# Two graph-attention layers on one core: the last scores moved behind the first attention, and one product given a bank of its own

## The chip, the core and the metric

The kernel runs on one core of a Trainium2 chip. The metric is the device time of one execution in microseconds (us), as the median of several runs. All times below are us unless they are marked ns. The engines are TensorE (PE for matmuls, PEld for loading the stationary operand), VectorE (DVE), ScalarE (ACT), GpSimd (POOL) and SyncE (SP). SP and ScalarE both issue transfers.

## The reference, cut to what matters

There are 64 graphs of 256 nodes with 512 features. The first layer mixes the features of each graph's nodes with a softmax over masked sums, and the second is an attention with 8 heads, biased by the logarithm of the adjacency.

```python
# layer 0
feat_proj = einsum('bnh,oh->bno', feats, fc_w) + fc_b
logits = q + swapaxes(k, 2, 1)                  # q, k: one number per node
masked = logits + (1.0 - adj_mat) * NEG_INF
masked = where(masked >= 0, masked, 0.01 * masked)
x1 = einsum('bnm,bmh->bnh', softmax(masked), feat_proj) + feats
# layer 1, heads of 64
Q, K, V = x1 @ W_q + b_q, x1 @ W_k + b_k, x1 @ W_v + b_v
scores = einsum('bihd,bjhd->bhij', Q, K) / sqrt(64)
scores = scores + soul_bias + log(adjacency + 1e-9)
out = einsum('bhij,bjhd->bihd', softmax(scores), V) + x1
```

Everything is float32.

## The kernel before

**Groups and steps.** Two graphs make a group (512 tokens), and there are 32 groups. The kernel is a software pipeline over groups: one `step` works on up to four of them at once. `d` is the group whose outputs are being finished, `a` the one in layer 1's attention, `f` the one that goes through layer 0's last part and the projections Q, K and V, and `n` the next one, for which weights of layer 0 are prepared. The function `attention_and_layer_0` holds the first half of a step and exists in 31 of the 32 steps. The order of the work is written out by hand as strings of names, each naming a method of a group: `A("scores:2 attend:0")` calls `scores(2)` and `attend(0)` of group `a`. Each engine, and the queue of transfers on SP and on ScalarE, executes its own instructions in exactly the order in which these calls issue them.

**Products.** Each of the four 512x512 projections (`pf` with fc_w, `pq`, `pk`, `pv`) is done by a scheme with seven products of half-size blocks (p1 to p7) in place of eight. A product is four matmuls of 128x128 by 128x256 (`add`, L412). They accumulate in few PSUM banks: in `r` products 1, 6, 5 and 3 follow each other, and between them ScalarE copies the partial sums to SBUF (`keep`). For `pf` (class `Mixed`), `keep` multiplies by the reciprocal of a softmax sum on ScalarE (L494) and POOL then adds the old x (L495). `sum` (L501 in `Mixed`, L443 elsewhere) adds a bank to what was kept and writes one quarter of the result, on VectorE: `sum_00`, `sum_11`, `sum_01`, `sum_10`. For `pf` the result is x1, written over x.

**The way of x1 to TensorE.** The projections need x1 transposed. Each quarter (o,k) of x1 goes this way. `send:o:k` transposes 32x32 blocks on VectorE into `xt` (L771) and writes `xt` to a scratch tensor `xd` in device memory by one transfer of 256 KB on SP (L775). `fetch:o:k` reads it back in a permuted order into `x1T` by four transfers of 64 KB on SP (L789), and `fetch_by_both:0:1` issues two of its four on ScalarE. `copy:0` copies the quarter (0,0) of `x1T` into `t1b_c` on ScalarE (L378), and `pv.p1` uses this copy as its stationary operand. `xsum:0` to `xsum:3` write the differences of quarters that products 4 to 7 need (`t1b`, L375, VectorE). `pq.p6` needs the second one, `xsum:1`, and that needs the quarters (0,0), (0,1) and (1,1).

**Layer 1's attention.** A group has four pieces of scores (u = 0 to 3, two for each graph). `scores:u` computes them (L843), and ScalarE applies the exponential (L857, `e`, six buffers). `factor:u:j` multiplies by the adjacency (L863, VectorE), and `both:u` adds two tiles for the softmax sums (L870). `attend:g` multiplies by V of graph g (L883), and `totals_g` sums (L910). The matmuls of scores have a contraction of 64, those of attend and totals 64 output rows; two of them share the array at a time. In the page's rows their operands read 64*128 and 128*64, against 128*128 for a product. The text calls a run of such matmuls between products a divided cluster. `turn`, `ratios`, `divide`, `complete` and `store` finish the output; `parts` prepares the sums. `keys` computes four rows of dot products of x1 on VectorE (L516), after which `load_x` may overwrite x with the next group's (SP, L206).

**PSUM.** Four banks are handed out by `bank` and two pairs of banks by `pair`, which scores and product 7 of `pq` use. A tile gets a bank once its last user has released it, so a matmul that starts a tile waits for the engine that read the bank last.

Of the kernel before, what the change touches and what calls it, by code (L numbers as in the profile page):

```python
# [25 lines left out]
def kernel(  # L26
# [86 lines left out]
    both = [i for i, a in enumerate(act_sets.SETS) if a.name == "natural_log_exp_and_others"]  # L113
# [50 lines left out]
    def fast():  # L164
        main = ExitStack()
        with main:
# [222 lines left out]
            class Product:  # L389
# [5 lines left out]
                scores = False  # L395
# [75 lines left out]
                def p3(self):  # L471
                    self.add(3, self.r, False)
                    self.read(self.out(0, 1), self.r, 0)
# [7 lines left out]
            class Mixed(Product):  # L481
# [22 lines left out]
                        )  # L504

                def p3(self):
                    self.add(3, self.r, False)

                def sum_01(self):
                    self.sum(0, 1, self.r, self.out(0, 1))  # L510


            def dot_rows(src, w_row, init, dst, name):
# [526 lines left out]
            def attention_and_layer_0(D, A, F, X, check):  # L1040

                A("scores:0")
                D("attend:1 totals_1")
                F("add_tiles")
                A("scores:1 factor:0:0 factor:0:1 pv.sum_11 pv.p3 pv.p4")
                D("ratios:1 turn:1")
                F("parts_0")
                A("factor:1:0 factor:1:1 pv.sum_10 both:0 both:1")
                check()
                F("mix:0 mix:1 ysum:0 recip")  # L1050
                D("divide:1 complete:1 store:1")
                A("residual:1")
                F("mix:2 mix:3 ysum:1 ysum:2 ysum:3")
                A("parts:0")
                F("pf.p1 pf.keep_1 pf.p2 pf.p6 pf.sum_00 begin send:0:0 fetch:0:0")
                A("turn_residual:1 parts:1")
                F("pf.p7 pf.p5")
                A("scores:2 attend:0 totals_0")
                F("pf.sum_11 send:1:1 fetch:1:1")
                A("factor:2:0 factor:2:1 turn:0")  # L1060
                F("pf.p3 pf.sum_01 send:0:1 pq.p1 pq.keep_1 copy:0 fetch_by_both:0:1")
                A("ratios:0 both:2")
                F("pf.p4 pf.sum_10 send:1:0")
                A("scores:3")
                F("fetch:1:0")
                A("factor:3:0")
                F("pk.p1 pk.keep_1 pv.p1 pv.keep_1")

            def check_ranges():

                in_range(NG - NR // 2, NG, "last")
                pk = bank("pok")
                nc.tensor.transpose(pk[0:1, 0:P], checked["all"], ident)

                def flag_ready():
                    oks = one.tile([1, 2], F32, tag="oks", name="oks")
                    nc.vector.tensor_reduce(oks[:, 0:1], pk[0:1, 0:P], AX.X, ALU.min)
                    nc.vector.tensor_copy(flag, oks[:, 0:1])

                return flag_ready  # L1080
# [3 lines left out]
            def step(d, a, f, n, check):  # L1084


                def of(group):
                    def issue(pieces):
                        for piece in pieces.split():
                            name, *args = piece.split(":")  # L1090
                            if group is None:
                                continue
                            target = group
                            if "." in name:
                                part, name = name.split(".")
                                target = getattr(group, part)
                            getattr(target, name)(*map(int, args))
                    return issue

                D, A, F, X = of(d), of(a), of(f), of(n)  # L1100
                X("load_adj")
                if a is not None:
                    attention_and_layer_0(D, A, F, X, check)
                else:
                    f.features_first()
                    F("pq.p1 pq.keep_1 copy:0 pk.p1 pk.keep_1 pv.p1 pv.keep_1")
                F("xsum:0 xsum:1 xsum:2 pq.p6 keys:2 keys:3 keys:0 keys:1")
                X("load_x")
                A("factor:3:1 both:3")
                F("pq.p7 pq.p2 pq.sum_00 xsum:3 pq.p5 pk.p6 pq.sum_11 pq.p3")  # L1110
                A("divide:0")
                X("dot_q:0 dot_q:1 dot_q:2 dot_q:3 spread")
                F("pq.p4 pq.sum_10 copy:1 copy:2")
                A("complete:0 store:0 parts:2")
                if n is None:
                    A("parts:3")
                F("pk.p7 pk.p5 pk.sum_11 residual:0")
                X("adjt")
                F("pk.p2 pk.sum_00")
                X("dot_k:0 dot_k:1")  # L1120
                F("pk.p3 pk.p4 pk.sum_10")
                X("dot_k:2 dot_k:3")
                F("turn_residual:0")
                if n is None:
                    A("attend:1 totals_1 ratios:1 turn:1 divide:1 complete:1 store:1")
                    F("residual:1 turn_residual:1")

                    F("pv.p2 scores:0 pv.p6 pv.sum_00 factor:0:0 factor:0:1 scores:1 both:0 pv.p7")
                    F("factor:1:0 factor:1:1 both:1 scores:2 pv.p5 sums_1:0 scores:3 pv.sum_11")
                    F("ratios_t:0 ratios_r:0 factor:2:0 factor:2:1 pv.p3 pv.p4 factor:3:0 pv.sum_10")  # L1130
                    F("factor:3:1 attend:0 finish:0 sums_of_e:1 attend:1")
                    F("ratios_t:1 ratios_r:1 finish:1")
                    check_ranges()()
                    return
                X("mask add_eps")
                F("pv.p2 pv.p6")
                X("weights:0")
                F("pv.p7 pv.p5")
                X("weights:1")
                F("pv.sum_00")  # L1140
                A("parts:3")

            with tc.manual_schedule(engines=ENGINES):
                f = Group(0)
                f.x, f.a = x_0, adj_0

                warm = bank("warm")
                for n in range(6):
                    nc.tensor.matmul(warm[:, 0:P], lhsT=ident, rhs=ident, start=True, stop=True)
                columns(rows_0, cols_0, "cols_0")  # L1150
                rows_qk = rows_of_x()
                k_constant = constant()
                d, a, a_w = None, None, {}
                for g in range(NG):
                    n = Group(g + 1) if g + 1 < NG else None

                    def check():

                        if d is not None and (d.g % NR == NR - 1 or d.g == NG - NR // 2 - 1):
                            in_range(d.g // NR * NR, d.g + 1, f"{d.g}")  # L1160

                    step(d, a, f, n, check)
                    d, a, f = a, f, n
# [215 lines left out]
```

## Time and profile before

| | before |
|---|---|
| median of 3 runs | 2327.16 (2326.76 to 2327.59) |
| profiled execution, its own time | 2324.43 |
| span of the profiled execution | 2322.6 |
| TensorE clock granted | 0.998 of full |
| TensorE with a matmul under way | 2302.7 (99%) |
| VectorE busy | 2092.7 (90%) |
| ScalarE busy | 1071.0 (46%) |
| POOL busy | 122.0 (5%) |
| DMA engines, mean busy share of q1 and q10 | 28.5% and 0.8% |

In the profile a matmul's recorded end overlaps the start of the next, so its cost is read from one start to the next. A float32 matmul appears as two records of PE and two of PEld. A row of the timeline gives the start, the duration of the merged records, the engine, the line, the operation and its tiles; in brackets stands how long the engine was idle before it, and what ended that. SPq and ACTq are the issue of transfers.

### The profile page before, as it was taken

Reading aid. Unit: us, or ns where it says so; the run is one execution under the profiler, and the core shown is the slowest. Engines: PE = TensorE matmul, PEld = TensorE weight load, DVE = VectorE, ACT = ScalarE, POOL = GpSimd, SP = SyncE. Lnnn points to the kernel's source line nnn. Section 1 sums busy time; section 2 is a strip of 40 time slices with the busy share of each in tenths; the row PEclk is TensorE's granted clock in tenths of the full one; section 3 lists DMA queues with packets and bytes.
Section 4 is the critical chain, followed back from the end, with each engine's and each line's share of the span. In section 5 each row is a group of like instructions: output and inputs, shape, how many; then the busy total and the mean of one; then the engine's idle time right before and its main releaser. Section 6 shows DMA issues by size and latency. Waiting matters only on the chain.

```text
span 2322.6 us, 33706 instructions
## 1 busy us (share of the span) xinstructions
PE 2302.7 (99%) x12738; PEld 1906.0 (82%) x12738; DVE 2092.7 (90%) x3088; ACT 1071.0 (46%) x1865; POOL 122.0 (5%) x120
## 2 busy tenths in 40 slices
PE   9999999999999999999999999999999999999997
PEld 5888888888888888888888888888888888888885
DVE  6799889999899998999999999999999989999897
ACT  3544445444444444454444444444544445444443
POOL 0000000000000000000000000000000000000000
PEclk9999999999999999999999999999999999999999
DMA  4122323223322323232233223322222323323312
GB/s 132 48 59 72 78 75 67 64 66 84 79 73 56 68 73 78 73 69 60 69 80 84 64 61 67 80 78 73 64 60 73 78 74 68 64 64 85 79 46 38
DMA packets 517263, 163.84 MB, mean 71 GB/s; under 512 B 415188, under 2 KB 478696, under 8 KB 517096
## 3 DMA queue, kind: packets, MB, share of 16 engines
q1 hardware_dynamic: 505512, 156.25, 28.5%
q10 hardware_dynamic: 11584, 5.38, 0.8%
q8 instruction: 103, 1.69, 0.3%
q14 instruction: 64, 0.52, 0.1%
HBM read 95.43 MB, written 66.12 MB: 70 GB/s over the span
## 4 chain that ended last, share of the span: by engine, by line
PE 95%; DVE 2%; DMA 2%; issue 0%; ACT 0%; ACTq 0%; DVEq 0%
PE pv L412 17%; PE pq L412 16%; PE pk L412 16%; PE pf L412 16%; PE sc L843 10%; PE oT L883 10%; PE y L667 9%; DMA x1T<-xd 1%; DMA xd<-xt 1%; PE fp L696 1%; DVE t1b L375 0%; DMA fc_nat<-in_L_gnn_fc_w_dram 0%; PE tot L910 0%; DVE xt L771 0%; PE rc L621 0%
## 5 line engine op out<-in xcount | busy, mean ns | idle before, releaser
L863 DVE TENSOR_TENSOR e<-e,am 128x1024 f32<-128x1024 f32 x254 | 300.5, 1214 | 24.1 <-ACT e L857 24.1
L857 ACT ACTIVATE e<-sc,c 128x1024 f32<-128x1024 f32 x254 | 269.0, 1110 | 77.0 <-PE sc L843 73.5
L843 PE MATMUL sc<-qT,kT 64*128 64x256 f32 x2048 | 255.8, 389 | 0.4 <-ACT e L857 0.4
L883 PE MATMUL oT<-e,v 128*64 128x256 f32 x2032 | 233.4, 382 | 0.0
L495 POOL TENSOR_TENSOR pf_s<-pf_s,x 128x512 f32<-128x512 f32 x93 | 118.5, 1274 | 2118.7 <-ACT pf_s L494 1673.4
L843 PEld LDWEIGHTS sc<-qT,kT 64*128 64x128 f32 x2048 | 187.2, 186 | 51.5 <-issue 31.5
L667 PE MATMUL y<-e,x 128*128 128x256 f32 x992 | 226.1, 382 | 0.0
L883 PEld LDWEIGHTS oT<-e,v 128*64 128x64 f32 x2032 | 140.2, 137 | 85.4 <-issue 21.3
L432 ACT ACTIVATE pq_s<-pq,cols 128x256 f32<-128x256 f32 x192 | 80.5, 470 | 279.1 <-PE pq L412 279.1
L667 PEld LDWEIGHTS y<-e,x 128*128 128x128 f32 x992 | 186.1, 190 | 24.0
L494 ACT ACTIVATE pf_s<-pf,recip 128x256 f32<-128x256 f32 x186 | 77.9, 470 | 197.6 <-PE pf L412 197.6
L900 DVE TENSOR_REDUCE part<-est 128x32 f32<-128x1024 f32 x124 | 151.3, 1220 | 4.3
L899 DVE STREAM_TRANSPOSE est<-es 128x1024 f32<-128x1024 f32 x124 | 152.2, 1227 | 0.0
L870 DVE TENSOR_TENSOR es<-e,e 128x1024 f32<-128x1024 f32 x126 | 149.3, 1205 | 1.1
L673 ACT COPY yT<-y 128x512 f32<-128x512 f32 x124 | 72.6, 586 | 131.5 <-PE y L667 130.8
L890 ACT COPY oTs<-oT 128x512 f32<-128x512 f32 x128 | 75.0, 586 | 119.1 <-PE oT L883 98.4
L429 ACT COPY pk_s<-pk 128x512 f32<-128x512 f32 x96 | 56.3, 586 | 151.9 <-PE pk L412 151.9
L412 PE MATMUL pk<-x1T,wk 128*128 128x256 f32 x512 | 124.2, 385 | 0.0
L412 PE MATMUL pk<-t1b,wk 128*128 128x256 f32 x512 | 121.1, 379 | 0.4 <-DVE kT L443 0.4
L412 PE MATMUL pv<-wv,t1b_c 128*128 128x256 f32 x512 | 121.1, 379 | 0.0
L412 PE MATMUL pv<-wv,t1b 128*128 128x256 f32 x512 | 121.1, 379 | 0.0
L412 PE MATMUL pq<-x1T,wq 128*128 128x256 f32 x512 | 121.0, 379 | 0.0
(180 smaller groups left out, 4474.7 us busy)
## 6 DMA issues: line engine op xcount, KB each, us to landing
x<-in_x_dram SPq DMA_DIRECT2D x32, 1024.0 KB, 5.1
out_dram<-osb SPq DMA_DIRECT2D x254, 128.0 KB, 3.3
xd<-xt SPq DMA_DIRECT2D x124, 256.0 KB, 2.0
x1T<-xd SPq DMA_DIRECT2D x434, 64.0 KB, 1.9
adj<-in_adj_dram SPq DMA_DIRECT2D x128, 128.0 KB, 3.5
qrow<-q SPq DMA_DIRECT2D x31, 256.0 KB, 3.9
x1T<-xd ACTq DMA_DIRECT2D x62, 64.0 KB, 2.4
fc_nat<-in_L_gnn_fc_w_dram ACTq DMA_DIRECT2D x4, 256.0 KB, 3.8
```

Source lines behind the costliest of these rows:

```text
L412: nc.tensor.matmul(o, lhsT=lk[:, ts(m, P)] if len(lk.shape) == 2 else lk[:, m], rhs=rk, start=(start and m == 0 and k == 0), stop=(m == 1 ...
L432: nc.scalar.activation(dst[:, m], src[:, m], AF.Identity, bias=self.bias[:, 2 * o + m : 2 * o + m + 1],)
L494: nc.scalar.mul(s[:, m], src[:, m], self.recip[:, TPG * k + m : TPG * k + m + 1])
L495: nc.gpsimd.tensor_tensor(s, s, self.out(o, k), ALU.add)
L667: nc.tensor.matmul(y[:, ts(gr, N)], lhsT=self.x[:, gr * TPG + j, ts(c, P)], rhs=self.e0[:, j, gr, :], start=(gr == 0 and j == 0), stop=(gr ...
L843: nc.tensor.matmul(sc[:, par, pr, :], lhsT=self.kT[rows, 2 * hg + pr, ts(t, P)], rhs=self.qT[rows, 2 * hg + pr, ts(gr, N)], start=True, st ...
L857: nc.scalar.activation(e, sc, AF.Exp, bias=self.c[:, t : t + 1], scale=SCALE)
L863: nc.vector.tensor_tensor(ef, ef, self.am[:, jc, u // 2, :].unsqueeze(1).to_broadcast([P, 4, N]), ALU.mult,)
L870: nc.vector.tensor_tensor(self.esum[u], self.e[u, 0], self.e[u, 1], ALU.add)
L883: nc.tensor.matmul(oT[par * HD : (par + 1) * HD, pr, :], lhsT=self.v[:, gr * TPG + jc, ts(h, HD)], rhs=self.e[2 * gr + hg, jc][:, par, pr, :],
L899: nc.vector.transpose(turned, self.esum[u].rearrange("p a b i -> p (a b i)"))
L900: nc.vector.tensor_reduce(self.part[:, hg, :], turned.rearrange("p (m c) -> p m c", c=B), AX.X, ALU.add,)
```

## The change

Three things are edited, all in the order of a step.

1. `pf.p3` no longer accumulates onto `r`, but starts a bank of its own, `r3`, and moves from behind `totals_0` to directly behind `pf.p5`, ahead of `scores:2`. The quarter (0,1) of x1 then takes two passes of `sum`: `add_01` adds the bank `r`, and `sum_01` adds `r3`. `add_01` stands ahead of `sum_11`.
2. `scores:3` moves up from behind `pf.p4` to directly behind `totals_0`. `pf.p4`, `pq.p1`, `pk.p1` and `pv.p1` follow it without another cluster between them. With this move `fetch_by_both:0:1` stands ahead of `scores:3` and of `pq.keep_1` and `copy:0` on ScalarE, where it had stood behind `copy:0`. `sum_01 send:0:1` move ahead of `factor:2:0` on VectorE, `send:1:1 fetch:1:1` ahead of `scores:2`.
3. `factor:3:0`, `factor:3:1` and `both:3` now stand together behind `xsum:2` and ahead of `keys`. Before, `factor:3:0` stood ahead of `xsum:0`, and the other two behind `keys`.

```diff
                 def p3(self):
-                    self.add(3, self.r, False)
+                    self.r3 = self.fresh(3)
+
+                def add_01(self):
+                    self.sum(0, 1, self.r, self.out(0, 1))
 
                 def sum_01(self):
-                    self.sum(0, 1, self.r, self.out(0, 1))
+                    self.sum(0, 1, self.r3, self.out(0, 1))
...
                 A("turn_residual:1 parts:1")
-                F("pf.p7 pf.p5")
+                F("pf.p7 pf.p5 pf.p3 pf.add_01 pf.sum_11 send:1:1 fetch:1:1")
                 A("scores:2 attend:0 totals_0")
-                F("pf.sum_11 send:1:1 fetch:1:1")
-                A("factor:2:0 factor:2:1 turn:0")
-                F("pf.p3 pf.sum_01 send:0:1 pq.p1 pq.keep_1 copy:0 fetch_by_both:0:1")
-                A("ratios:0 both:2")
-                F("pf.p4 pf.sum_10 send:1:0")
-                A("scores:3")
-                F("fetch:1:0")
-                A("factor:3:0")
-                F("pk.p1 pk.keep_1 pv.p1 pv.keep_1")
+                F("pf.sum_01 send:0:1 fetch_by_both:0:1")
+                A("factor:2:0 factor:2:1 scores:3 turn:0 ratios:0 both:2")
+                F("pf.p4 pf.sum_10 send:1:0 fetch:1:0")
+                F("pq.p1 pq.keep_1 copy:0 pk.p1 pk.keep_1 pv.p1 pv.keep_1")
...
-                F("xsum:0 xsum:1 xsum:2 pq.p6 keys:2 keys:3 keys:0 keys:1")
+                F("xsum:0 xsum:1 xsum:2 pq.p6")
+                A("factor:3:0 factor:3:1 both:3")
+                F("keys:2 keys:3 keys:0 keys:1")
                 X("load_x")
-                A("factor:3:1 both:3")
                 F("pq.p7 pq.p2 pq.sum_00 xsum:3 pq.p5 pk.p6 pq.sum_11 pq.p3")
```

## The prediction

> **What bounds the kernel.** I read the busy table first, then TensorE's waits, then one undisturbed step of the timeline, engine by engine.
>
> ```profile
> PE 2302.7 (99%) x12738; PEld 1906.0 (82%) x12738; DVE 2092.7 (90%) x3088; ACT 1071.0 (46%) x1865; POOL 122.0 (5%) x120
> PE pq L412 <- DVE t1b L375: 3.3, 6, 1.3
> q8 instruction: 103, 1.69, 0.3%
> ```
>
> TensorE has work in 99% of the span, so a gain must come from its own instruction stream, or from its few waits. The list of waits holds one that recurs: six times the pq product 6 waits for a difference of x1 pieces (t1b), which waits for a transfer. TensorE's timeline of one step, and next to it ScalarE's, SP's and VectorE's:
>
> ```profile
> 740.53 1.89 PE L412 MATMUL pf<-fcT,tb 128*128 128x256 f32 x8
> 742.35 2.00 PE L843 MATMUL sc<-qT,kT 64*128 64x256 f32 x16
> 744.28 3.67 PE L883 MATMUL oT<-e,v 128*64 128x256 f32 x32
> 747.78 0.26 PE L910 MATMUL tot<-part,every 128*64 128x32 f32 x4
> 747.97 1.99 PE L412 MATMUL pf<-fc_s,yT 128*128 128x256 f32 x8
> 749.80 1.89 PE L412 MATMUL pq<-x1T,wq 128*128 128x256 f32 x8
> 751.53 1.89 PE L412 MATMUL pf<-fcT,tb 128*128 128x256 f32 x8
> 753.35 2.00 PE L843 MATMUL sc<-qT,kT 64*128 64x256 f32 x16
> 755.28 1.99 PE L412 MATMUL pk<-x1T,wk 128*128 128x256 f32 x8
> 757.11 1.89 PE L412 MATMUL pv<-wv,t1b_c 128*128 128x256 f32 x8
> ```
> ```profile
> 751.73 0.84 ACT L432 ACTIVATE pq_s<-pq,cols 128x256 f32<-128x256 f32 x2 [3.14 <-PE pq L412]
> 752.46 0.62 ACT L378 COPY t1b_c<-x1T 128x512 f32<-128x512 f32 x1
> 753.72 0.85 ACTq L789 DMA_DIRECT2D x1T<-xd  x2
> 754.62 2.12 ACT L857 ACTIVATE e<-sc,c 128x1024 f32<-128x1024 f32 x2 [1.55 <-PE sc L843]
> ```
> ```profile
> 746.33 0.34 SPq L775 DMA_DIRECT2D xd<-xt  x1
> 748.40 1.73 SPq L789 DMA_DIRECT2D x1T<-xd  x4
> 751.65 0.34 SPq L775 DMA_DIRECT2D xd<-xt  x1
> 753.72 0.78 SPq L789 DMA_DIRECT2D x1T<-xd  x2
> ```
> ```profile
> 744.68 0.88 DVE L501 SCALAR_TENSOR_TENSOR x<-pf,recip,pf_s 128x256 f32<-128x256 f32 x2 [0.89 <-POOL pf_s L495]
> ```
>
> (q8: packets, MB, share of the DMA engines.) See in TensorE's rows the distance from start to start, since ends overlap. A product takes 1.73 (749.80 to 751.53). The last product before a divided cluster takes 1.82 (740.53 to 742.35), the first one after it 1.83 (747.97 to 749.80). So each divided cluster costs 0.09 + 0.10 = 0.20 at its edges (0.198 from the records in ns). Most steps repeat every 71.16.
>
> **What the Trainium skill says.** The Trainium skill, "TensorEngine Tiling (Array Packing)", Key Properties: a change of tiling mode drains TensorE. The 0.09 and 0.10 agree. The same skill, "PSUM — Partial Sum Buffer", Engine vs sequencer instructions: ScalarE's queue is a strict FIFO. In the fourth step of this trace ScalarE stands 3.46 behind one late xd transfer, with the exponentials of the scores behind it. And "Runtime: NRT & Kernel Launch", Instruction fetch mechanics: instructions come by DMA in 16 KiB blocks of 256, mostly hidden. Here q8's packets are 16,384 bytes, some 23 us apart, one per 256 TensorE records; they are hidden from TensorE, but not from transfers in flight, as shown below.
>
> **The change, part by part.** Everything is laid on the clock of the step above.
>
> 1. Two clusters instead of three. After: p5 740.53, p3 742.26, scores 2 744.08, attend 746.01, totals 749.51, scores 3 749.70, p4 751.63, pq.p1 753.46, pk.p1 755.18, pv.p1 756.91, pq.p6 758.64 (758.83 before). No matmul is added or removed; one cluster's edges go: 31 steps x 0.198 = **-6.1**.
>
> 2. The banks. p3 takes a bank that TensorE itself freed. attend then needs VectorE's sum_00 (done 739.5, needed 746.0) and the new add_01 (744.65, needed 747.8), totals needs sum_01 (747.1, needed 749.5), scores 3 needs the exponentials of scores 2 (746.3 and 747.4, needed 749.7). Margins of 2 us and more: 0.
>
> 3. add_01: two more VectorE instructions of L501, 0.88 a pair. They run from 743.8 to 744.65, inside the 0.89 in which VectorE waits for POOL. Without that cover send:1:1 would be 0.9 later. Cost 0; sum_11 and its transposition stay at 744.68 and 745.59.
>
> 4. Differences before the last factors. xt of piece (0,1) is ready at 747.85 instead of 751.6. SP, however, issues in order: the four fetches of (1,1) end at 750.13, so xd follows at 750.17, only 1.5 earlier than before. It lands 2.06 later, 752.2; the fetches land by 755.1, and the second difference, for which pq.p6 waits, is done at 756.6 instead of 758.3, with 1.8 to spare instead of 0.5. The six waits, 4.3 and 0.10 of restart each by the records, should go: **-4.9**.
>
> 5. factor:3 and both:3 ahead of keys: VectorE ends keys at 763.5 instead of 761.7, and load_x on SP starts 1.75 later. It lands 5.1 later, 768.7, where VectorE wants it at 768.4. The 0.3 is lost in the 1.1 that the first kT sum has before pk.p4 needs it. Cost 0, at most 0.1 a step.
>
> 6. ScalarE's place for the two fetches. Before they stood behind pq.keep_1 and copy:0, and ahead of scores 3 only. Now they stand ahead of the exponentials of scores 3, pq.keep_1 and copy:0, and **pv.p1 loads its weights from what copy:0 writes**. ScalarE waits until 752.2, issues for 0.85, and runs the exponentials 753.12 to 755.24; it can take pq.keep_1 at 755.15, where pq.p1 is done at 755.38: **0.24 to spare**. Then copy:0 ends at 755.38 + 1.35 = 756.73 (751.73 to 753.08 took 1.35), and pv.p1 can bear a load up to 756.80, less 0.05 of signalling (both seen where TensorE waited for VectorE). In a quiet step this costs 0, by 0.02.
>
> 7. In a step that isn't quiet, xd of (0,1), or the transfers of (1,1) ahead of it on SP, are late, and nearly all of it reaches TensorE. Set against the times of q8's packets, the late transfers are those that met one. Twelve xd writes that did so took 0.9 to 2.0 more than 2.06 (mean 1.3); five sets of four fetches took 0.5 to 1.5 more to issue (mean 0.9). The exposed stretch now runs from xd of (1,1) to ScalarE's second fetch, 746.3 to 753.1. By TensorE's records it holds some 115 of 256, as small matmuls go by fast there: 115/256 x 31 = 14 steps. At 0.9 (hits at the edges cost less) minus 0.2 to spare: 14 x 0.7 = **+9.8**. Bounds: the delays that this trace has on the same transfers, less the slack, give 7.0 with half of the stretch empty; I take 5 as the low end, and 15 x 1.15 = 17 as the high end.
>
> Sum: -6.1 - 4.9 + 9.8 = -1.2. The profiled execution took 2324.4 (span 2322.6); it would take 2323.2. The median of the runs is 2.7 higher, so I forecast **2326.0**. About 0.2%, 4.65 us, is what a measurement of this kernel can tell from no change.
>
> **Rivals.**
> (a) Likeliest: gains and ScalarE's new wait cancel. With the term of 7 between 6.4 and 15.6 the result lies within 4.65: 2322.5 to 2331.8. Chance 0.50.
> (b) The wait is harmless: q8's packets fall elsewhere, as the order moved, or hold up less. With 5 or less left: -6, 2321; with nothing left -11, 2316. For it: before, only 9 of 31 steps had a delay of over 0.24 on these transfers. Against it: the stretch is longer, and denser in TensorE records. Chance 0.24.
> (c) Slower: xd of (0,1) now goes out 0.04 behind the last fetch of (1,1), not 1.5 behind it. Were it later by 0.45 in every step, the slack of 7 (0.2) would be gone: 31 x 0.25 + 14 x 0.2 = 10.6 on top of -1.2, 2336.6. It turns the sum to over +4.65 from 0.3 late. Against it: xd of (1,0), issued 0.55 behind ScalarE's last fetch, lands in 2.03 as ever, and the fetch's packets need only some 0.1 per DMA engine where they overlap. A term of 7 at its high end gives +6, 2333, as well. Chance with that 0.21.
> (d) The edges aren't drains of a mode change but belong to each product's neighbours, so that the merged cluster pays them inside. Against it: from totals to scores takes 0.19 where the step has that order already (720.82 to 721.01), as from totals to a product (747.78 to 747.97). Without the 6.1 it is +4.9, 2332. Chance 0.05.
>
> Range for 8 in 10: 2319.5 to 2334. Faster 0.24, same 0.50, slower 0.26 (c and d).
>
> **What would show it.** Right: TensorE's product after totals gone, one 1.82 and one 1.83 fewer per step, quiet steps of 70.96; no wait of pq for t1b; in its place waits of pv L412 for ScalarE's t1b_c, some 14 of 0.2 to 1.7; ScalarE idle before its exponentials for xd. Wrong: quiet steps of 71.16 (d), a wait at pv.p1 in every step (c), or fewer than eight (b); a wait at attend, totals or pk.p4 would break 2 or 5.

## The result, and the profile after

| kernel | median of the runs | against before, 95% interval |
|---|---|---|
| before | 2327.16 (2326.03 to 2328.91, 9 runs) | |
| changed | 2335.34 (2329.86 to 2339.79, 9 runs) | 1.0034 [1.0025, 1.0042] |

The change makes the kernel slower by 8.2 us, where 2326.0, within the noise of before, was forecast; it lies above the range of 2319.5 to 2334. The profiled execution took 2335.59 (span 2333.8), 11.2 more than that of before; 3.4 of this lie in the start-up, which the change does not touch (the first step begins at 78.84 instead of 75.46, and at 75.71 in a second profile of the changed kernel). The thirty steps from the first start to the last are 7.75 longer, so it is the steps that must explain the result.

The page of the changed kernel, busy times, queues and two groups of instructions (busy, mean ns, then the idle time ahead of them and what ended most of it):

```profile
PE 2305.7 (99%) x12738; PEld 1912.6 (82%) x12738; DVE 2114.1 (91%) x3150; ACT 1069.7 (46%) x1865; POOL 124.1 (5%) x120
q8 instruction: 103, 1.69, 0.3%
L860 ACT ACTIVATE e<-sc,c 128x1024 f32<-128x1024 f32 x254 | 268.5, 1108 | 190.2 <-PE sc L846 80.3
L412 PE MATMUL pv<-wv,t1b_c 128*128 128x256 f32 x512 | 124.6, 387 | 11.5 <-ACT t1b_c L378 11.3
```

Its list of waits (us in total, times, longest):

```profile
ACT e L860 <- DMA xd<-xt: 71.3, 21, 4.9
PEld pv L412 <- ACT t1b_c L378: 18.4, 19, 2.5
PE pv L412 <- ACT t1b_c L378: 11.3, 10, 2.1
```

The wait of pq for t1b is gone from the list. In its place pv L412 waits for t1b_c, in its weight loads and in its matmuls, and ScalarE's exponentials (L860) now wait for xd. (ScalarE's wait for xd was 3.5, once, before.) The place is the one the prediction named; the size is not. Taken from TensorE's records, pq.p6 starts later behind pk.p1 than in a quiet step, by 17.5 in sum, in 18 steps of 31; nearly all of it is lost at pv.p1, and I call it the delay at pv.p1 (only the 21st step, with 3.98 the longest, loses some 1.6 of it at pq.p6). The forecast was 9.8.

TensorE's timeline of a quiet step of the changed kernel, the tenth, the same as was shown of before:

```profile
743.76 1.89 PE L412 MATMUL pf<-fcT,tb 128*128 128x256 f32 x8
745.49 1.89 PE L412 MATMUL pf<-fc_s,yT 128*128 128x256 f32 x8
747.31 2.00 PE L846 MATMUL sc<-qT,kT 64*128 64x256 f32 x16
749.23 3.67 PE L886 MATMUL oT<-e,v 128*64 128x256 f32 x32
752.74 0.26 PE L913 MATMUL tot<-part,every 128*64 128x32 f32 x4
752.92 2.00 PE L846 MATMUL sc<-qT,kT 64*128 64x256 f32 x16
754.85 1.99 PE L412 MATMUL pf<-fcT,tb 128*128 128x256 f32 x8
756.68 1.89 PE L412 MATMUL pq<-x1T,wq 128*128 128x256 f32 x8
```

Add 3.23 to the starts of item 1 and they are these, to 0.01. The quiet step is 70.97, not 71.16. ScalarE's timeline of that step, and SP's:

```profile
755.61 0.85 ACTq L792 DMA_DIRECT2D x1T<-xd  x2
756.51 2.12 ACT L860 ACTIVATE e<-sc,c 128x1024 f32<-128x1024 f32 x2 [2.97 <-DMA xd<-xt]
758.61 0.84 ACT L432 ACTIVATE pq_s<-pq,cols 128x256 f32<-128x256 f32 x2
759.34 0.62 ACT L378 COPY t1b_c<-x1T 128x512 f32<-128x512 f32 x1
```
```profile
749.56 0.34 SPq L778 DMA_DIRECT2D xd<-xt  x1
751.63 1.73 SPq L792 DMA_DIRECT2D x1T<-xd  x4
753.46 0.38 SPq L778 DMA_DIRECT2D xd<-xt  x1
755.61 0.78 SPq L792 DMA_DIRECT2D x1T<-xd  x2
```

xd of (0,1) goes out at 753.46 and ScalarE issues its fetches 2.15 later; copy:0 (t1b_c) is done at 759.96, and pv.p1 starts at 760.14, where an undelayed step has it. So a quiet step pays nothing, as item 6 had it. The loss sits in the other steps, and there are two kinds of these.

**Steps that meet a packet of instructions.** The seventh step, on ScalarE, SP and TensorE:

```profile
542.56 0.85 ACTq L792 DMA_DIRECT2D x1T<-xd  x2
543.46 2.12 ACT L860 ACTIVATE e<-sc,c 128x1024 f32<-128x1024 f32 x2 [4.75 <-DMA xd<-xt]
...
546.18 0.63 ACT L378 COPY t1b_c<-x1T 128x512 f32<-128x512 f32 x1
```
```profile
534.72 0.34 SPq L778 DMA_DIRECT2D xd<-xt  x1
538.49 1.73 SPq L792 DMA_DIRECT2D x1T<-xd  x4
540.32 0.38 SPq L778 DMA_DIRECT2D xd<-xt  x1
```
```profile
543.58 1.89 PE L412 MATMUL pk<-x1T,wk 128*128 128x256 f32 x8
546.86 1.99 PE L412 MATMUL pv<-wv,t1b_c 128*128 128x256 f32 x8 [1.39 <-ACT t1b_c L378]
```

xd of (1,1) takes 3.77 instead of 2.07 (534.72 to 538.49); a packet of q8 started 0.7 behind its issue. All that follows on SP is 1.7 late, ScalarE gets its two fetches out 1.8 late, and pv.p1, which would start 1.73 behind pk.p1, starts 3.28 behind it. This is item 7, as written.

**Steps with a range check.** Every fourth step VectorE checks reciprocals ahead of ysum:0, six small instructions of some 1.6 (ok, okp, L1033 to L1040). Both kernels do it, and the prediction does not speak of it. VectorE, GpSimd and SP around the 25th step, where no packet of q8 comes near:

```profile
1806.34 0.17 DVE L1033 TENSOR_SCALAR ok<-recip 128x16 f32<-128x16 f32 x1
...
1807.88 0.16 DVE L1040 TENSOR_TENSOR okp<-okp,okp 128x1 f32<-128x1 f32 x1
1807.96 0.69 DVE L350 TENSOR_TENSOR tb<-yT 128x512 f32<-128x512 f32 x1
...
1811.02 0.69 DVE L350 TENSOR_TENSOR tb<-yT,tb 128x512 f32<-128x512 f32 x1
1811.62 0.68 DVE L350 TENSOR_TENSOR tb<-yT 128x512 f32<-128x512 f32 x1
1812.22 1.76 DVE L350 TENSOR_TENSOR tb<-yT,tb 128x512 f32<-128x512 f32 x1
...
1822.12 0.86 DVE L501 SCALAR_TENSOR_TENSOR x<-pf,recip,pf_s 128x256 f32<-128x256 f32 x2
```
```profile
1811.96 1.47 POOL L495 TENSOR_TENSOR pf_s<-pf_s,x 128x512 f32<-128x512 f32 x1 [62.79 <-ACT pf_s L494]
```
```profile
1823.76 0.34 SPq L778 DMA_DIRECT2D xd<-xt  x1
1825.83 0.30 SPq L792 DMA_DIRECT2D x1T<-xd  x1
```

No idle time stands ahead of any of these VectorE instructions. The last sum of y pieces meets GpSimd's add and takes 1.76, where it takes 0.69 otherwise. xd of (1,1), the transfer that send:1:1 issues ("the send" below), leaves 7.74 behind the start of pf.p5, where a quiet step has 5.80, and pv.p1 is delayed by 1.79. In the eight steps with a check (5, 9, 13, 17, 21, 25, 29 and 31) the send is late by 0.26 to 1.94 in this profile, and the delays of these steps are 11.6 of the 17.5, some with a packet's part in them. In the profile of before it is at 5.80 in every step from the second on. VectorE of before ahead of ysum:0 and ysum:1 in the tenth step, and ahead of sum_11 in the 25th, which has a check:

```profile
730.77 0.69 DVE L350 TENSOR_TENSOR tb<-yT 128x512 f32<-128x512 f32 x1 [0.70 <-ACT yT L673]
734.44 0.69 DVE L350 TENSOR_TENSOR tb<-yT,tb 128x512 f32<-128x512 f32 x1 [0.53 <-ACT yT L673]
...
1813.83 0.88 DVE L501 SCALAR_TENSOR_TENSOR x<-pf,recip,pf_s 128x256 f32<-128x256 f32 x2 [0.79 <-POOL pf_s L495]
```

The idle time ahead of ysum:0 (0.80 in most steps without a check) takes half of the check, and the 0.53 ahead of ysum:1 most of the rest. Both are gone in a step with a check (0.14 is left in the 31st); the wait of 0.89 ahead of sum_11 is still 0.76 to 0.90 there.

Where the idle time ahead of ysum:0 went is seen 47 instructions and 32 us earlier, in the quiet step again. VectorE of the changed kernel, and of before:

```profile
770.45 1.22 DVE L986 TENSOR_TENSOR osb<-osb,recip 128x1024 f32<-128x1024 f32 x1
773.07 0.69 DVE L519 CUSTOM_DVE_ANT_0 jq<-x,wq_row 128x512 f32<-128x512 f32 x1 [1.41 <-DMA x<-in_x_dram]
```
```profile
767.47 1.22 DVE L983 TENSOR_TENSOR osb<-osb,recip 128x1024 f32<-128x1024 f32 x1
768.60 0.69 DVE L516 CUSTOM_DVE_ANT_0 jq<-x,wq_row 128x512 f32<-128x512 f32 x1
```

VectorE now waits 1.41 for the load of x, since that load starts later; what it does not do in this time, it has to do ahead of ysum:0 of the next step, where it has no idle time at all after the tenth step.

### The profile page after: what moved, and what is told of

Same layout as the page of the kernel before. It is cut to its first block, busy times and chain, and to the rows that moved or that the text cites. A ratio compares the mean times of both kernels' runs of the same rounds, so it can differ in the third digit from the quotient of the medians.

```text
span 2333.8 us, 33829 instructions
## 1 busy us (share of the span) xinstructions
PE 2305.7 (99%) x12738; PEld 1912.6 (82%) x12738; DVE 2114.1 (91%) x3150; ACT 1069.7 (46%) x1865; POOL 124.1 (5%) x120
## 5 line engine op out<-in xcount | busy, mean ns | idle before, releaser
L860 ACT ACTIVATE e<-sc,c 128x1024 f32<-128x1024 f32 x254 | 268.5, 1108 | 190.2 <-PE sc L846 80.3
L495 POOL TENSOR_TENSOR pf_s<-pf_s,x 128x512 f32<-128x512 f32 x93 | 120.5, 1296 | 2127.8 <-ACT pf_s L494 1999.6
L412 PE MATMUL pv<-wv,t1b_c 128*128 128x256 f32 x512 | 124.6, 387 | 11.5 <-ACT t1b_c L378 11.3
L412 PE MATMUL pk<-t1b,wk 128*128 128x256 f32 x512 | 121.3, 380 | 1.3 <-DVE kT L443 1.3
L412 PEld LDWEIGHTS pv<-wv,t1b_c 128*128 128x128 f32 x512 | 95.6, 192 | 32.0 <-ACT t1b_c L378 18.4
L412 PE MATMUL pv<-wv,t1b 128*128 128x256 f32 x512 | 121.1, 380 | 0.0
L412 PE MATMUL pk<-x1T,wk 128*128 128x256 f32 x512 | 121.0, 379 | 0.0
```

Of the source, the lines that this page charges most:

```text
L412: nc.tensor.matmul(o, lhsT=lk[:, ts(m, P)] if len(lk.shape) == 2 else lk[:, m], rhs=rk, start=(start and m == 0 and k == 0), stop=(m == 1 ...
L495: nc.gpsimd.tensor_tensor(s, s, self.out(o, k), ALU.add)
L860: nc.scalar.activation(e, sc, AF.Exp, bias=self.c[:, t : t + 1], scale=SCALE)
```

## Experiments

The theory going in: two causes of about the same size, ScalarE's wait exposed to q8's packets (item 7), and VectorE's lateness in the check steps (items 5 and 3 without their cover). Rivals: packets alone; the transfers themselves, whichever engine issues them; add_01. The runs were made on several chips; the kernel before had a median of 2325.8 to 2326.9 beside them, and each ratio is against the runs of before on the same chip. "Keys late" is the order of the changed kernel, "keys first" that of the first experiment.

### keys and load_x back ahead of the factors (e2_keys_first)

```diff
-                A("factor:3:0 factor:3:1 both:3")
                 F("keys:2 keys:3 keys:0 keys:1")
                 X("load_x")
+                A("factor:3:0 factor:3:1 both:3")
```

> keys and load_x again ahead of factor:3:0, factor:3:1 and both:3; all else as in the changed kernel. Theory (load_x 1.75 later has taken VectorE's idle time ahead of ysum, which before covered the range check of every fourth step): jq starts 1.2 earlier, VectorE has its 0.8 of idle before ysum back, send of (1,1) is late by at most 0.5 in the steps with a check instead of 0.3 to 1.9, and no sum of y pieces meets POOL's add; the waits of pv.p1 fall from 17.5 to 9 to 12. Time 2327 to 2331. Rival (item 5 costs nothing, as forecast; the lateness in the check steps comes from add_01 alone): send of (1,1) is as late as in the changed kernel, 2334 to 2337.

Measured: 2326.24 (21 runs), 0.9997 [0.9990, 1.0004]. VectorE in the 25th step:

```profile
1803.23 0.16 DVE L1040 TENSOR_TENSOR okp<-okp,okp 128x1 f32<-128x1 f32 x1
1803.31 0.68 DVE L350 TENSOR_TENSOR tb<-yT 128x512 f32<-128x512 f32 x1
...
1807.57 0.69 DVE L350 TENSOR_TENSOR tb<-yT,tb 128x512 f32<-128x512 f32 x1
```

jq starts 1.4 earlier in a quiet step, 27.89 behind p5 instead of 29.31, and without a wait. ysum:0 has 0.77 of idle time in steps without a check, no sum of y pieces is held up, and the send of (1,1) is at 5.80 in all steps (5.86 in the first). Moving these three pieces gives back the whole 9. The delays at pv.p1 fall to 13.8 in this profile, not to the 9 to 12 expected, while the time is 1 better than expected. The fall is where it should be: the eight steps with a check have 5.2 instead of 11.6. The other 23 have 8.6 instead of 5.9, so the part of the packets differs by some 3 from one profile to another. What is left is item 7.

### The range checks left out (e3_no_check, e10_keys_no_check)

```diff
-    if d is not None and (d.g % NR == NR - 1 or d.g == NG - NR // 2 - 1):
+    if d is not None and d.g == NG - NR // 2 - 1:
```

Once in the changed kernel, and once with keys first as well.

> Leaves out the range check of the reciprocals in seven of its eight places (those of every fourth graph; the one near the end stays). Theory (two causes of the waits at pv.p1: VectorE late by the check, and TensorE's instruction packets): send of (1,1) is at 5.80 after p5 in all steps but the last, and the waits at pv.p1 fall by the share of the steps 5, 9, 13, 17, 21, 25 and 29 that the packets do not explain, 6 to 8; what is left, 9 to 11, is what the prediction priced at 9.8. Time 2327 to 2330. Rival (the packets cause all of it, the late send in those steps is another effect of them): 2334 to 2336.

> Keys and load_x ahead of the factors of scores 3, and seven of the eight range checks left out. Theory (the check costs time only because the late load_x has taken the idle time that covered it; either edit alone gives back the same 9): no more than either alone, 2324 to 2327. Rival (two separate costs that add): 2316 to 2319.

| | check kept | seven checks left out |
|---|---|---|
| keys late (the change) | 2335.34, 1.0034 [1.0025, 1.0042] | 2325.51, 0.9999 [0.9991, 1.0008] |
| keys first | 2326.24, 0.9997 [0.9990, 1.0004] | 2326.43, 1.0005 [0.9997, 1.0013] |

Either edit alone gives back 9; both together give no more. So neither the check nor the late keys has a price that can be told without the other: the loss is the check in a place whose idle time was given away. e3 was expected at 2327 to 2330 and came out 1.5 below that. The delays at pv.p1 in the two profiles without checks are 8.5 and 11.9, of them 3.4 and 4.6 in the eight steps of the checks.

### One part alone in the kernel before (b3_keys_late, b2_bank_add)

In b3 factor:3:1 and both:3 go ahead of keys in the kernel before (its factor:3:0 stays ahead of xsum:0). In b2 product 3 gets its bank and add_01 stands ahead of sum_11; nothing moves.

> The kernel before with one part of the change alone: factor:3:1 and both:3 ahead of keys and load_x. Theory (VectorE's late send in the check steps costs time only where ScalarE's wait stands ahead of pv.p1): send of (1,1) is late by up to 1 in the check steps, and xd of (0,1) still leaves at 5.3 after it by p3; 2326 to 2329, the same as before. Rival 1 (VectorE without idle time ahead of ysum costs 9 by itself): 2333 to 2337. Rival 2 (load_x some 2.3 later makes jq and with it kT late for pk.p4 in every step): 31 times 0.3 or more, 2336 or above.

> The kernel before with the bank of its own for product 3 and add_01 alone; order and clusters as before. Theory (add_01 takes the 0.89 that VectorE waits for POOL, and the bank is free in time): 0, 2325.5 to 2328; in the check steps the send of (1,1) is late by some 0.3 at most, without a cost, as in the kernel with keys late alone. Rival (add_01 is part of the lost 9): 2329 or above.

Measured: b3 2327.60, 1.0004 [0.9998, 1.0011]; b2 2327.56, 1.0004 [0.9996, 1.0012]. Neither costs anything that can be told. In b3 VectorE does lose its idle time ahead of ysum, and the send of (1,1) is late by 1.0, 1.0 and 1.2 in steps 5, 9 and 25. It costs little (pq.p6 is late by 0.7 in these three steps together), since xd of (0,1) follows the late product 3 anyway, and pv.p1 does not stand behind ScalarE's fetch. In the other five steps with a check the wait ahead of sum_11 takes up the lateness: 0.11 to 0.21 of it is left. In b2 the send stays at 5.80 and add_01 is as free as item 3 said. The changed kernel has both edits, and there the send is late in all eight steps. How much of the 9 is due to add_01, and how much to item 6's new path, was not tested apart.

### Four fetches on SP (e1_sp_fetch), and with keys first (e5_sp_keys)

```diff
-                F("pf.sum_01 send:0:1 fetch_by_both:0:1")
+                F("pf.sum_01 send:0:1 fetch:0:1")
```

> All four fetches of piece (0,1) are issued by SP; ScalarE issues none. Theory (ScalarE's two fetches, standing ahead of the exponentials, pq.keep_1 and copy:0, carry every late transfer to pv.p1): the waits of pv.p1 for t1b_c, 17.5 in the changed kernel's profile, vanish; x1's last fetch ends 0.85 later, so that the second difference has some 0.9 to spare before pq.p6 instead of 1.8, and only delays above 0.9 reach TensorE there, 2 to 5 in sum. Time 2335.3 - 17.5 + 2 to 5 = 2320 to 2323, faster than before by 4 to 7. Rival 1 (the late transfers themselves cost the time, whichever queue issues): the wait moves from pv.p1 to pq.p6 with its size, 2331 to 2336. Rival 2 (VectorE's own lateness in the steps with a range check costs the time, not through ScalarE): some 8 of the 17.5 stay, at pq.p6 or pk.p4, 2327 to 2330.

> Both edits together: all four fetches of piece (0,1) on SP, and keys and load_x ahead of the factors of scores 3. With SP alone and load_x late, the second difference of x1 was 0.85 later, jq waited for x 22 more, and pk.p4 waited for kT in nearly every step (+0.6). Theory (VectorE's place is what SP's longer queue cost there: load_x 1.75 earlier gives it back): the waits at pk.p4 go, the waits at pv.p1 stay away, and what is left are some ten waits of 0.2 to 1.6 at pq.p6, 8 in sum: 2326.2 - 13.8 + 8 = 2319 to 2323. Rival (0.85 more on the second difference is itself too much for VectorE, whose order then runs late to pk.p4 in any case): 2330 to 2336.

Measured: e1 2341.25, 1.0063 [1.0050, 1.0077]; e5 **2316.65**, 0.9959 [0.9945, 0.9972]. The first is slower than either kernel, which none of its theories had. Waits of e1, then of e5:

```profile
DVE jq L519 <- DMA x<-in_x_dram: 53.9, 30, 2.5
PEld pk L412 <- DVE kT L443: 21.7, 24, 1.3
PE pk L412 <- DVE kT L443: 12.4, 18, 0.9
PE pq L412 <- DVE t1b L375: 6.5, 8, 1.4
```
```profile
PEld pq L412 <- DVE t1b L375: 1.9, 5, 0.6
PE pk L412 <- DVE kT L443: 0.4, 1, 0.4
PE pq L412 <- DVE t1b L375: 0.2, 1, 0.2
```

pv.p1 waits no more in e1, but VectorE loses 1.9 of each step waiting for x (median; 1.0 in the changed kernel) and has next to no idle time ahead of ysum:0 (0.04 at most after the first step), so that its lateness comes out at pk.p4 and pq.p6. The send is 1.8 to 2.0 late in seven of the steps with a check, and pq.p6 is late by 7.4 in sum in these steps, without any wait of ScalarE. A likely reading, not tested apart: while TensorE stood at pv.p1, VectorE caught up, and with that wait gone it does not. The queue alone is not to blame: e5 has the same SP queue, VectorE has its 0.79 ahead of ysum back, and 24.6 go with the move of keys (24 by the ratios). Nor is the second difference 0.85 later by it, as the expectation had. From the issue of xd of (0,1) to its end it takes 7.05 (median of the 31 steps, in e1 and in e5), against 6.65 to 6.71 in the changed kernel and in e2.

e5 beats both kernels, and its own range by 2.3: pq.p6 starts late by 0.8 in sum, where 8 were expected. It is about what the edges and the six waits are worth: 11.0 were forecast for items 1 and 4, and 10.2 came.

### GpSimd's queue for ScalarE's two fetches (e7_pool_keys)

With keys first, nc.gpsimd takes the place of nc.scalar in fetch.

> GpSimd's queue in place of ScalarE's for two of the four fetches of piece (0,1); keys and load_x ahead of the factors of scores 3. Theory (it is ScalarE's place in front of its exponentials, not the transfers, that makes late transfers cost time): pv.p1 waits for t1b_c no more; SP still issues two fetches only, so that the second difference keeps its 1.8 to spare, less what GpSimd needs for a DMA issue, which no trace here shows; up to 1.5 more is harmless: 2312 to 2318, faster than before by 9 to 14. Rival (GpSimd's issue takes over 2 us): pq.p6 waits in every step, 31 times 0.5 or more, 2330 or above.

Measured: 2320.46, 0.9973 [0.9965, 0.9981]. ScalarE's wait is gone here too; the second difference is done 7.16 behind the issue of xd of (0,1) (median), later than with either other choice, and pq.p6 waits in five steps, 5, 7, 15, 23 and 31, by 0.8 to 1.6. The time is 2.5 above the range expected.

### The packets shifted (e4_warm128, e8_warm64, e9_warm32)

Small matmuls are added at the very start of the changed kernel, to move q8's packets against the steps:

```diff
+                for n in range(32):
+                    nc.tensor.matmul(warm[:, 0:4], lhsT=ident, rhs=ident[:, 0:4], start=True, stop=True)
```

> 128 more matmuls of 128x4 on TensorE at the very start, half of the 256 records between two of TensorE's instruction packets; the start-up takes up to 10 more. Theory (the waits outside of the check steps come where such a packet meets the transfers of (1,1) and (0,1)): the steps with a wait outside of the checks, now 4 to 7, 12 to 15, 19 and 20, 27 to 30, move by three to five steps and leave 6, 14, 20 and 28 quiet; their sum stays within 5 to 12. Rival (something in the order of the steps themselves delays the transfers): the same steps wait.

> 64 more matmuls of 128x4 at the very start of the changed kernel. A matmul makes two records (128 more matmuls were 256 more records, one whole block, and the same steps waited as without them), so that these are 128, half a block; the start-up takes 28 more. Theory (a wait outside of the check steps comes where a packet of TensorE's instructions meets the transfers of (1,1) and (0,1)): the steps that wait move by half the cycle of 7 to 8 steps: quiet are 6, 14, 20 and 28, and waits come at some of 1 to 3, 9 to 11, 16 to 18, 23 to 26. Rival: the same steps wait as before the edit, 4 to 7, 12 to 15, 19 to 21, 27 to 30.

> 32 more matmuls of 128x4 at the start of the changed kernel. The records of the runs with 64 and 128 more show why those moved nothing: each matmul is two records of TensorE and two of its weight loads, 64 of them 256 instructions and one more packet (103, 104, 105 packets), so that these two edits were one and two whole cycles. 32 are half a cycle; the start-up takes 12 to 14 more. Theory (outside of the check steps a wait comes where a packet of TensorE's instructions meets the transfers of (1,1) and (0,1)): the steps that met packets at 0 to 6 after xd of (1,1), 4 to 7, 12 to 15, 20 to 23, 28 to 31, move by about four; 6, 7, 14, 15, 28 and 30 are quiet, and waits come at some of 1 to 3, 8 to 11, 16 to 19, 24 to 27. Rival (the steps themselves delay the transfers): the same steps wait.

The first two were laid out on a wrong count: a matmul of float32 is four instructions, two matmuls and two weight loads, and 64 of them are exactly one packet more (103, 104 and 105 packets with 0, 64 and 128). So they moved nothing, and nearly the same steps waited. Half a packet moved them, as the third expectation had it: the steps it named as quiet are quiet, and the delays come in steps that it named. The delay at pv.p1, and how far behind the issue of xd of (1,1) the nearest packet began, from the traces:

```
step       1    2    3    4    5    6    7    8    9   10   11   12   13   14
changed
 delay     0    0    0   .04 1.39  .86 1.66   0   .28   0    0   .18 2.09  .31
 packet    -    -    -   5.7  3.5  2.1  0.7 -0.9   -    -    -   5.8  1.8  1.7
64 more
 delay     0    0    0   .29 1.63  .15 1.07   0   .36   0    0  1.99 1.21   0
 packet    -    -    -   6.0  3.4  1.9  0.7 -0.6   -    -    -   5.1  3.4  1.6
32 more
 delay   1.53  .75 1.52   0   .34   0    0    0  2.52  .57 1.64   0   .44   0
 packet   4.8  2.4  1.1 -1.1   -    -    -   5.6  2.0  2.3  0.8   -    -    -
```

The delays go with the packets, four steps earlier. What stays in place are the check steps 5, 9 and 13, with a packet or without. (The times of these three kernels, 2388.93, 2358.85 and 2347.09, the last two of one run each, are mostly those of a start-up longer by the added matmuls, and nothing is read from them.)

### The changed kernel again (e11_changed)

> The changed kernel once more, for its share of the waits at pv.p1 in a second profile: 2333 to 2337. Theory: the send of (1,1) is late in the check steps alone (5, 9, 13, 17, 21, 25, 29, 31), by 0.3 to 2, and their waits are 9 to 13 of some 17; the waits of the other steps come in the same steps as in the first profile, with other sizes. Rival (the late sends were an accident of the first profile): late in other steps, or in none.

Measured: 2334.88, 1.0041 [1.0028, 1.0055]. The send is late in the same eight steps and in no other, by 0.27 to 1.97; the delays at pv.p1 are 17.2, of them 11.9 in the check steps.

## Why the prediction was wrong

The step that failed is the "Cost 0" of item 5, together with that of item 3. From the first step to the last, before and changed, the sum can be read in the traces: item 1 gave -5.9, item 4 gave -5.0, the delays at pv.p1 are 17.2 instead of item 7's 9.8, and 1.5 is lost elsewhere, most of it at pk.p4 in the 27th step: +7.8 in all. Two thirds of the delays are in the steps with a check, and either leaving these out or moving the keys back takes away 9.

- **Item 1 held**, with rival (d) out: 70.97, and no edge inside the merged cluster.
- **Item 2 held**: no wait at attend or totals, and at scores one of 0.3, as before (0.4).
- **Item 4 held**: no wait of pq for t1b is left. With item 1 it is what e5 shows alone, 10.2 of the 11.0.
- **Item 6 held**, narrowly. xd of (0,1) took 2.15 in the tenth step, not 2.06, and the step is not delayed. Rival (c) was wrong in its mechanism; its 2336.6 comes near the result by another road.
- **Item 7 held in kind and nearly in size**. With VectorE on time the delays are 13.8 (e2), 8.5 (e3) and 11.9 (e10), against 9.8 within 5 and 17. By the times, e2 is 9.6 above e5, in which this path is gone (8.8 by the ratios). The half-packet shift shows the cause. That 14 delays are over 0.2 in the changed kernel, as forecast, is luck: eight of them are those of the steps with a check.
- **Item 5 failed.** It put the late load of x at "lands 5.1 later, 768.7, where VectorE wants it at 768.4", and let the 0.3 be lost. On the same clock VectorE wanted it at 768.4, and it was used at 769.84: keys ended 0.24 later than worked out, and the load took 5.96 from its issue to its use instead of 5.1. So 1.4 was lost in the tenth step, not 0.3. More than the size, the bookkeeping failed. The item looked for cover ahead of the next kT sum and stopped there (pk.p4 did wait, by 1.3 in two steps, against 0.4 in one before). But VectorE of that step works without a break from jq on, and the idle time lost there was missing 32 later, ahead of ysum:0, where the check needs it.
- **Item 3 held alone, but not beside item 5.** The 0.89 ahead of sum_11 pays for add_01, and in before nothing else draws on it: 0.76 or more of it is left even in a step with a check. With the keys late, the check draws on it too (0.7 to 0.9 in b3), and in the changed kernel add_01 has spent it. The prediction read a quiet step only and never listed what the steps with a check do there.

This is the 9 that is missing. With keys first the time is 2326.24 where 2326.0 was forecast; that it comes so near is partly luck, since item 7's part alone differs by some 5 between the profiles.

The list of what would show the prediction wrong named waits at attend, totals and pk.p4, and the count at pv.p1. It named no lateness of the send of (1,1), which item 7 takes for fixed at 746.3.

## What to carry to other kernels

An idle stretch on an engine off the critical path is a budget: write down everything that draws on it, in the rarest kind of step as well as in the commonest, before an edit is costed at nothing because the stretch covers it. When two edits are free alone (late keys and add_01, each in the kernel before), price them together: here one took the idle time that covered the check, and the other took the reserve behind it. And a wait that is removed may have been what let another engine catch up (e1 suggests it), so look for the next engine in line before expecting the whole of it back.

## What the runs showed of the hardware

**VectorE and GpSimd shut each other out, in one pair of instructions.** The last sum of y pieces (tb, L350, both inputs in SBUF) met GpSimd's add (L495) 32 times within 0.35 of each other's start, in the two profiles of the changed kernel, e1 and b3. In the 16 meetings where it began 94 to 346 ns behind the add, it took 1.76, always, instead of 0.69. In the 16 where it began first, or up to 28 ns behind, it took 0.68 or 0.69, and the add 1.47 to 1.85 instead of 1.28. The Trainium skill, "SBUF — State Buffer", Who interferes with whom, says that a VectorE instruction with two SBUF inputs contends with a GpSimd instruction that reads SBUF, for a shared pair of ports that only one of them holds at a time. The trace agrees. In each of the first 16 meetings the sum before the last one was still running when the add began, so the trace reads as the add waiting for that one (it took 1.30 to 1.56) and the last sum for the add: in all 32 the add ended 1.81 to 1.83 behind the start of one sum, here the earlier, in the other 16 the last. Other instructions of VectorE beside the same adds (part, est, xt, x) kept their durations. In the changed kernel this turns a lateness of 0.8 in a check step into one of 1.9, in three of the steps in each profile.

**A second queue for four fetches gains less than the issues that it saves.** With two fetches on SP and two on ScalarE the second difference was done 0.35 to 0.4 earlier than with four on SP (medians of 31 steps: 6.65 to 6.71 behind the issue of xd of (0,1) in the changed kernel and e2, 7.05 in e1 and e5), though two issues take 0.8 and four 1.7: ScalarE's fetches land in 2.4 (median), SP's in 2.0. With two on GpSimd, which land in 2.2, it was 7.16.

**One packet of q8 is 64 matmuls of float32.** A transfer that meets its 16 KiB can be delayed: xd of (1,1) took 3.77 instead of 2.07 in the seventh step, and 4.13 in the 30th step of e8. Where the packet falls in a step moves with what stands ahead of it: 32 matmuls more at the start shifted the delayed steps by four, 64 more left them in place.
